# A four-layer graph network, layer 1's second attention turned key-major, the output bias added by DMA, and launch's tests put behind the samples

## The chip, the cores and the metric

The kernel runs on one core of a Trainium2 chip. Such a core has five engines that run side by side and meet at semaphores: TensorE (PE, matmuls and transposes; its weight loads are listed as PEld), VectorE (DVE), ScalarE (ACT), GpSimd (POOL) and SyncE (SP, which here only issues DMAs). Each engine works through its own list of instructions strictly in order. The metric is the time of one execution in microseconds. Before the change the median of three runs is 4023.1 us (4022.46 to 4024.0).

## The reference

32 samples, each a matrix x of 512 nodes by 256 features, go one after the other through four residual layers. All share one 512x512 adjacency. Each layer adds a graph network of relu(layernorm(x)) to x:

```python
h = relu(layernorm(x)); x = x + L0(h)   # 4 heads: softmax over neighbours of q.k/8, then out @ wo.T + bo
h = relu(layernorm(x)); x = x + L1(h)   # relu(h @ mlp1), attention over all nodes, mlp2, attention over neighbours
h = relu(layernorm(x)); x = x + L2(h)   # 4 heads of additive attention, elu
h = relu(layernorm(x)); x = x + L3(h)   # 8 heads of additive attention with a prior, @ W_out.T
```

The change is about the additive attention of layer 1, `_gat(inp, adj, W, a)`:

```python
h = inp @ W;  f1 = h @ a[:F];  f2 = h @ a[F:]
e = leaky_relu(f1[i] + f2[j], 0.2);  e = -9e15 where adj[i, j] is 0
out = elu(softmax_j(e) @ h)
```

Layer 1 does it twice: `first_gat` without a mask on 512 features, `second_gat` with the mask on 256. Both results go through a second elu and get their input added.

## The kernel before, in words

All arithmetic is float32. A sample's 512 nodes are four tiles of 128 partitions (`NT = 4`), its 256 features two (`KD = 2`). A scratch tile of 128x512 is a *block* (57 of them in SBUF), and a PSUM tile of the same size a *bank* (8). A feature-major tile has features on its partitions and nodes along its row; a node-major tile has it the other way round.

**Launch (lines 424 to 601).** Loads go out on the queues of SP, ScalarE and GpSimd. The adjacency is converted to float and turned by 16 transposes (496). Four masks come from it. The projections of the attention vectors on the weights of layers 2 and 3 are computed (480 to 487), as are bias columns (566), `boa` (587, 595: output bias of layer 0, with the value bias carried through wo) and `b2a` (592, 596). *Tests* bound the sizes of the scores (524 to 582). Their verdict `go` is loaded into a register on every engine (1367), and a branch (1368) leads to `pipelined`, which runs here, or to `general`, a slower path for inputs that the bounds do not admit. The samples' own loads stand behind that branch.

**The samples (`pipelined`).** The code of the four layers doesn't issue instructions. A recorder (`q.vector`, `q.tensor` and so on) collects each operation as a step. `Plan.order` (156) then puts all steps of all samples into one order. For each step it works out the earliest start from the engine's time, from the steps that it depends on, from free blocks and banks, and from a release time (`STARTS`, `PACE`, `LAYERS`); among steps it takes the one with the earliest start and, between equals, the earliest due time: the sample's number times `PERIOD`, less the length of what hangs on the step, less a value out of `URGENT`. Durations in this planner come from `cost` (311). `issue` (265) emits the steps in that order, each on its engine, and beyond the first 100 steps slips in one of launch's leftovers (`late`: 8 products over W_fc, 4 over W_hand, 4 mask products) at every other step. So nearly every instruction of the samples carries one line, 275, in the profile, and is told apart by the tiles that it writes and reads. On TensorE, units of matmuls that use row halves or column strips of the array are kept together (`q.unit`).

**Layer 0 (733 to 779).** Norm, transposes, q, k and v; per head pair and key tile scores, an exponential, a mask product and running sums; then weighted sums. `normalise` (708) sends the sums through DRAM and back to get their reciprocals on all partitions. At 776 four GpSimd additions put `boa` onto x, and two VectorE additions add the product with wo.

**Layer 1, first attention (781 to 840).** It is key-major: a tile p[j] has the 128 keys of j on its partitions and all queries along its row. With d the largest f2 of all nodes, the softmax weight is a maximum of two products, each of a factor of the query and a factor of the key. The query's factor is put on all partitions by four transposes and a copy, the sums over keys are taken from a total by four transposes and a reduction, and their reciprocals are spread again by four transposes (`rc`).

**Layer 1, second attention (842 to 880).** It is query-major: queries on the partitions, keys along the row.

```python
q.tensor.transpose(fb[:, col(t)], v[:, t, D + 1 : D + 2].to_broadcast([P, P]), ident)   # f2 on all partitions
q.scalar.activation(s, fb, AF.Identity, bias=v[:, t, D : D + 1])                        # + f1
q.vector.scalar_tensor_tensor(s, s, ALPHA, s, op0=ALU.mult, op1=ALU.max)                # leaky relu
q.vector.tensor_tensor_reduce(out=p[t], in0=s, in1=mask1[:, t, :], ...)                 # mask, row minimum of -e
q.scalar.activation(p[t], p[t], AF.Exp, bias=nm[:, t : t + 1], scale=-1.0, accum_out=sm[:, t : t + 1])
q.vector.reciprocal(r[:, t : t + 1], sm[:, t : t + 1])
q.scalar.mul(p[t], p[t], r[:, t : t + 1])
```

The weighted sum needs keys on the partitions, so 16 transposes and four copies (pT, 864 to 868) turn p.

**Layers 2 and 3 (`separable`, 902).** Key-major; a query row R per head comes back from DRAM (rd) on all partitions. Per head and key tile there is one exponential on ScalarE and one masked maximum on VectorE. Part of the sums is added by accumulating DMAs that GpSimd issues (p<-p). The last samples take sums on TensorE instead (`direct`).

Of the kernel before, what the change touches and what calls it, by code (L numbers as in the profile page):

```python
# [39 lines left out]

PERIOD = 57.0
STARTS, PACE = (0.0, 11.0, 54.0, 70.0), 29.0
LAYERS = (0.0, 55.0, 178.0, 198.0)

URGENT = {
    "h:0": 49, "pt:0": 23, "mm:0": 7, "sc:0": 89, "p0:0": -655, "total:0": -158, "av:0": -3, "rc:0": -39,
    "oT:0": -103, "stats:1": 94, "h:1": 11, "pt:1": 6, "hT:1": 93, "mm:1": -5, "r1:1": -511, "total:1": -50,
    "rs1:1": -41, "av:1": -24, "o2:1": -243, "fb:1": -11, "s:1": 20, "r2:1": 94, "pt:2": 134, "mm:2": -7,  # L50
    "p3:2": -20, "av:2": -185, "total:2": -319, "sm:2": -35, "ue:2": -200, "stats:3": 6, "ms:3": -69,
    "h:3": -156, "hT:3": 112, "mm:3": -58, "e8:3": -19, "p3:3": -989, "av:3": -489, "total:3": -598,
    "raw:3": -11,
}
BLOCKS, KEEP = 57, 2
KEEP_BANKS = 0

LATE = 100
BANKS = ("mm", "av", "sm", "sc", "pt", "fb")
# [10 lines left out]
class Plan:  # L70
# [85 lines left out]
    def order(self):  # L156
# [16 lines left out]
        free = {tag: [0.0] * bufs for tag, (bufs, _) in self.tags.items()}  # L173
        held = {}
# [136 lines left out]
def cost(engine, op, args, kw, out):  # L311
# [22 lines left out]
    if engine == "POOL":  # L334
        if op == "dma_start":
            return 1.1, 5.2
        return (1.0 if n < 16 else 0.683), 0.1
# [7 lines left out]
def gnn_stack_kernel(ctx: ExitStack, tc: tile.TileContext, a: dict, out: bass.AP):  # L345
# [21 lines left out]
    def load_rows(name, eng, cols):  # L367

        src = a[name]
        k = src.shape[0] // P  # L370
        t = const.tile([P, k, cols], F32, name=name)
        eng.dma_start(t[:, :, : src.shape[1]], T(src, "(k p) c -> p k c", p=P))
        return t
# [5 lines left out]

    def load_bcast(pool, name, eng, n):  # L380
        t = pool.tile([P, n], F32, name=name)
        load(t, name, eng)
        return t
# [12 lines left out]
    go = const.tile([1, 1], I32, name="go")  # L396
    bq8 = const.tile([P, KD], F32, name="bq8")
# [11 lines left out]
    mask1 = const.tile([P, NT, N], BF16, name="mask1")  # L409
# [3 lines left out]

# [6 lines left out]
    afc = first.tile([P, 2 * HID], F32, name="afc")  # L420
    ahd = first.tile([P, 2 * D], F32, name="ahd")
    prf = first.tile([P, HID], BF16, name="prf")
# [3 lines left out]
    with prep_stack, tc.manual_schedule():  # L426
# [5 lines left out]
        nc.scalar.dma_start(w2[:, :, H2 : H2 + D], T(a["L2_W"], "(k p) c -> p k c", p=P))  # L432
        src = a["L2_a"]
        a2 = prep.tile([P, 2, F2], F32, name="a2")
        nc.scalar.dma_start(a2, bass.AP(tensor=src.tensor, offset=src.offset, ap=[[0, P], [1, 2 * F2]]))
        for k in range(KD):
            nc.gpsimd.dma_start(
                T(w3[:, k, H3 : H3 + D], "p (h f) -> p h f", h=H3), T(a["L3_W"][:, k * P : (k + 1) * P, :], "h p f -> p h f")
            )
        bt = load_bcast(prep, "beta", nc.scalar, 1)  # L440
# [8 lines left out]
        wq = load_rows("wqT", nc.scalar, D)  # L449
        wk = load_rows("wkT", nc.sync, D)  # L450
        s3 = load_bcast(prep, "L3_a_src", nc.sync, D)
        d3 = load_bcast(prep, "L3_a_dst", nc.sync, D)
        m2 = load_rows("mlp2_w", nc.sync, D)
        wo = load_rows("woT", nc.sync, D)
        bo = load_bcast(prep, "bo", nc.sync, D)
        wv = load_rows("wvT", nc.sync, D)
        m1 = load_rows("mlp1_w", nc.sync, HID)
        wfc = load_rows("W_fc", nc.sync, HID + 2)
        f1a, r1a = wfc[:, :, HID : HID + 1], wfc[:, :, HID + 1 :]
        load(afc, "a_fc", nc.sync)  # L460
        wh = load_rows("W_hand", nc.sync, D + 2)
        load(ahd, "a_hand", nc.sync)
        w3o = load_rows("L3_WoT", nc.sync, D)

# [4 lines left out]
        one = prep.tile([P, 1], F32, name="one")  # L469
        nc.vector.memset(one, 1.0)  # L470
        H = H2 + H3
        tests = prep.tile([P, 2 * H + 5], F32, name="tests")
        nc.vector.memset(tests, 0.0)


        def project(w, kn, heads, f, vec, dst):

            for k in range(kn):
                pr = prep.tile([P, heads, f], F32, name="pr")
                nc.vector.tensor_tensor(pr, T(w(k), "p (h f) -> p h f", h=heads), vec, op=ALU.mult)  # L480
                nc.vector.tensor_reduce(dst(k), pr, axis=AX.X, op=ALU.add)

        def projections(w, h, f, vs, vd):
            project(lambda k: w[:, k, h : h + D], KD, h, f, vs, lambda k: w[:, k, :h])
            project(lambda k: w[:, k, h : h + D], KD, h, f, vd, lambda k: w[:, k, 3 * h + D :])
            nc.vector.tensor_scalar(w[:, :, h + D : 2 * h + D], w[:, :, :h], ALPHA - 1.0, None, op0=ALU.mult)
            nc.vector.tensor_scalar(w[:, :, 2 * h + D : 3 * h + D], w[:, :, 3 * h + D :], ALPHA, None, op0=ALU.mult)


        top = prep.tile([P, NT], F32, name="top")  # L490
# [6 lines left out]
        at = [prep.tile([P, N], F32, name="at", bufs=NT) for _ in range(NT)]  # L497
        m3 = [mask3T[:, j, :] for j in range(NT)]
        for j in range(NT):
            nc.scalar.copy(at[j], adjT[j])  # L500
            nc.scalar.activation(m3[j], adjT[j], AF.Relu)
        projections(w2, H2, F2, a2[:, 0:1, :].to_broadcast([P, H2, F2]), a2[:, 1:2, :].to_broadcast([P, H2, F2]))

        ab = prep.tile([P, 1], F32, name="ab")
        nc.vector.tensor_scalar(ab, bt, -1.0, None, op0=ALU.mult)
        nc.vector.tensor_tensor(ab, ab, bt, op=ALU.max)
        nc.scalar.activation(ab, ab, AF.Exp, scale=-1.0)
        nc.scalar.activation(ab, ab, AF.Ln, bias=one)
        for j in range(NT):
            nc.scalar.activation(m3[j], m3[j], AF.Ln, bias=eps)  # L510
        projections(w3, H3, F3, T(s3, "p (h f) -> p h f", h=H3), T(d3, "p (h f) -> p h f", h=H3))
        nc.vector.scalar_tensor_tensor(beta, bt, 0.0, ab, op0=ALU.max, op1=ALU.add)

        grams = []
        for w, name in ((wq, "bq"), (wk, "bk")):
            gp = pp.tile([64, N], F32, name="gp", bufs=2)
            for h in range(4):  # L520
                c = slice(h * 64, (h + 1) * 64)
                r = row[:, spans[name] + h * 64 : spans[name] + (h + 1) * 64]
                for k in range(KD):
                    nc.tensor.matmul(gp[:, c], w[:, k, c], w[:, k, c], start=(k == 0), stop=False)
                nc.tensor.matmul(gp[:, c], r, r, start=False, stop=True)
            gram = prep.tile([64, D], F32, name="gram", bufs=2)
            nc.vector.tensor_copy(gram, gp[:, :D])
            grams.append(gram)
        gp = pp.tile([64, N], F32, name="gp", bufs=2)
        for n in range(2):  # L530
            for h in range(4):
                c = slice(h * 64, (h + 1) * 64)
# [892 lines left out]
```

## Time and profile before

| | |
|---|---|
| median of three runs | 4023.1 us |
| the profiled execution | 4023.19 us |
| its span, first to last instruction | 4021.3 us |
| granted TensorE clock, mean | 0.994 |
| the chain that ended last, shares of the span | products mm 30%, weighted sums av 19%, transposes pt 5% |
| largest work on VectorE | masked maxima of layer 3, 715.2 us in 1024 |
| HBM traffic | 44 GB/s over the span |

The profile is one execution. A line of groups gives the engine, the operation, the tile written and the tiles read, the shapes and the count; then the busy time of all and the mean duration of one in ns; then how long the engine sat idle just before them and which instruction ended that. A matmul of float32 data is listed as two records, a transpose as one. Records of TensorE overlap, so busy time over count says what one adds, and the mean what one takes from start to end. A table by stage has, for each stretch, its length, the busy time of PE, PEld, DVE, ACT and POOL with counts, the granted clock, the DMA share and GB/s.

### The profile page before, as it was taken

To read this page: it belongs to the slowest core of one execution; us is meant where nothing else is said; L and a number is where in the kernel's file an instruction comes from. 1 tells how busy PE (TensorE), PEld (TensorE's weight loads), DVE (VectorE), ACT (ScalarE), POOL (GpSimd) and SP (SyncE) were. 2 spreads that over 40 slices of the span, in tenths; PEclk is the share of its full clock that TensorE was granted. 3 is DMA by queue.
4 is the path that set the end of the run, shared out by engine and by line. 5 is a ranking of instruction groups with operands and counts; after the bars stand their busy time and mean duration, and the time that the engine had idled before them with its cause. 6 is when DMAs were issued, how large, how long until landed. Compare 5 with 4: busy or idle time off the path is not lost.

```text
span 4021.3 us, 53382 instructions
## 1 busy us (share of the span) xinstructions
PE 3933.0 (98%) x17366; PEld 2179.0 (54%) x17366; DVE 3303.2 (82%) x6940; ACT 2992.8 (74%) x6386; POOL 659.0 (16%) x636
## 2 busy tenths in 40 slices
PE   8999999999999999999999999999999999999997
PEld 4655555555555655555555555655555555555553
DVE  6478888788888888888788887888888788887877
ACT  4568687877788777877877788777877777787766
POOL 2101110212121021110211211021110211111110
PEclk9999999999999999999999999999999999999998
DMA  2003231323332132322322323133322322322331
GB/s 81 17 17 90 64 85 54 80 64 69 75 80 72 46 90 63 74 70 67 86 64 61 82 65 87 47 71 73 83 69 67 85 64 59 78 70 71 65 79 49
DMA packets 198018, 274.80 MB, mean 68 GB/s; under 512 B 47273, under 2 KB 84394, under 8 KB 197730
## 3 DMA queue, kind: packets, MB, share of 16 engines
q1 hardware_dynamic: 144832, 176.05, 14.2%
q0 software_dynamic: 52064, 94.66, 13.8%
q8 instruction: 139, 2.28, 0.2%
q14 instruction: 149, 1.22, 0.1%
q10 hardware_dynamic: 834, 0.59, 0.1%
HBM read 157.74 MB, written 19.10 MB: 44 GB/s over the span
## 4 chain that ended last, share of the span: by engine, by line
PE 60%; DVE 17%; ACT 5%; DMA 4%; POOL 3%; issue 2%; SPq 0%; DVEq 0%; ACTq 0%; POOLq 0%
PE mm L275 30%; PE av L275 19%; PE pt L275 5%; DVE p L275 4%; PE sm L275 3%; PE sc L275 3%; DVE total L275 3%; ACT p L275 2%; POOL rs L275 2%; DVE x L275 2%; DVE stats L275 2%; DMA p<-p 2%; DVE ue L275 2%; DVE o L275 1%; DMA rc<-s 1%
## 5 line engine op out<-in xcount | busy, mean ns | idle before, releaser
L275 ACT ACTIVATE p<-R,e 128x512 f32<-128x512 f32 x1536 | 1005.4, 731 | 108.0 <-PE av L275 73.7
L275 DVE SCALAR_TENSOR_TENSOR p<-p,e,mask3T 128x512 f32<-128x512 f32 x1024 | 715.2, 741 | 179.5 <-ACT p L275 179.0
L275 PE MATMUL av<-p,v 128*128 128x512 f32 (+1 forms) x2048 | 700.5, 597 | 2.6 <-DVE p L275 2.5
L275 POOL TENSOR_TENSOR rs<-ve,mhalf 128x4 f32<-128x4 f32 x128 | 216.3, 1689 | 2214.4 <-DVE ve L275 1761.9
L275 DVE TENSOR_TENSOR total<-total,p 128x512 f32<-128x512 f32 x808 | 527.6, 683 | 0.8
L275 PE MATMUL av<-p,vs 128*32 128x512 f32 (+1 forms) x3072 | 491.0, 598 | 5.3 <-DVE p L275 5.3
L275 POOL DMA_DIRECT2D p<-p x360 | 323.0, 1095 | 1049.3 <-DVE p L275 412.9
L275 PE MATMUL mm<-W_fc,o 128*128 128x256 f32 (+1 forms) x2048 | 482.0, 381 | 4.9 <-ACT o L275 4.7
L275 PEld LDWEIGHTS av<-p,v 128*128 128x128 f32 (+1 forms) x2048 | 256.1, 163 | 348.5 <-issue 299.4
L275 PEld LDWEIGHTS mm<-W_fc,o 128*128 128x128 f32 x2048 | 375.4, 190 | 88.9 <-ACT o L275 22.3
L275 DVE TENSOR_TENSOR p<-p,mask0T 128x512 f32<-128x512 f32 x512 | 329.5, 680 | 65.0 <-ACT p L275 65.0
L275 DVE SCALAR_TENSOR_TENSOR p<-p,e,mask1T 128x512 f32<-128x512 f32 x512 | 355.0, 742 | 4.6 <-ACT p L275 4.3
L275 ACT ACTIVATE h<-x,ms,rs 128x256 f32<-128x256 f32 x512 | 276.8, 602 | 76.1 <-DVE ms L275 67.8
L275 PEld LDWEIGHTS av<-p,vs 128*32 128x32 f32 (+1 forms) x3072 | 133.1, 118 | 323.8 <-issue 238.2
L275 DVE TENSOR_TENSOR total<-p,p 128x512 f32<-128x512 f32 x404 | 279.7, 710 | 12.3 <-DMA p<-p 7.6
L275 ACT COPY v<-mm 128x256 f32<-128x256 f32 (+2 forms) x384 | 170.0, 452 | 138.7 <-PE mm L275 107.0
L275 ACT ACTIVATE p<-sc 128x512 f32<-128x512 f32 x512 | 256.1, 618 | 15.7 <-PE sc L275 15.5
L275 PE MATMUL mm<-w,hT 128*128 128x272 f32 (+1 forms) x1024 | 253.7, 395 | 8.0 <-ACT hT L275 8.0
L275 PE MATMUL mm<-hT,mlp_w 128*128 128x512 f32 x512 | 242.2, 600 | 2.4 <-ACT hT L275 1.5
L275 PE MATMUL sc<-qT,kT 64*128 64x512 f32 x1024 | 241.1, 606 | 0.2 <-ACT p L275 0.2
L275 PE MATMUL mm<-o,mlp_w 128*128 128x512 f32 x512 | 238.0, 594 | 0.0
L275 PE MATMUL av<-pT,v 128*128 128x512 f32 x512 | 226.6, 593 | 0.1
(189 smaller groups left out, 5977.3 us busy)
## 6 DMA issues: line engine op xcount, KB each, us to landing
R<-rd SPq DMA_DIRECT2D x384, 256.0 KB
p<-p POOLq DMA_DIRECT2D x360, 256.0 KB, 5.3
x<-in_x_dram SPq DMA_DIRECT2D x32, 512.0 KB
rc<-s SPq DMA_DIRECT2D x128, 128.0 KB
out_dram<-x SPq DMA_DIRECT2D x32, 512.0 KB
rc<-s SPq DMA_DIRECT2D x248, 64.0 KB
s<-sums SPq DMA_DIRECT2D x94, 8.0 KB
few<-s SPq DMA_DIRECT2D x94, 8.0 KB
```

The lines of the kernel that those rows point to most:

```text
L275: getattr(getattr(self.nc, attribute), op)(*args, **kw)
```

## The change

The diff touches four things.

- **Second attention** becomes key-major like the first. `largest`, `on_all`, `inverse_sums` and `elu2` are taken out of `first_gat` and shared. The mask is the transposed one; the products with `rc` come after the weighted sums. A condition on the spread of f2 in each sample is new (`spread`).
- **Output bias**: one DMA per sample, issued by GpSimd, accumulates `boa` into x; it is held until v is written.
- **Launch**: only the adjacency, x of sample 0 and q, k and v are loaded ahead of the samples, and only two masks and the bias columns are made. All other loads and preparations (`preparation`) are slipped in between the samples' steps from the 30th on. The tests become steps of a 33rd sample of the plan (`tests`). The branch comes behind everything: `pipelined` always runs, and `general` runs behind it if the verdict is against.
- **The planner's numbers**: PERIOD, STARTS, PACE, LAYERS and URGENT, 62 blocks for 57, ten of them held back until its time 120.

```diff
-PERIOD = 57.0
-STARTS, PACE = (0.0, 11.0, 54.0, 70.0), 29.0
-LAYERS = (0.0, 55.0, 178.0, 198.0)
+PERIOD = 134.0
+STARTS, PACE = (0.0, 0.0, 82.0, 163.0), 113.0
+LAYERS = (0.0, 48.0, 0.0, 189.0)
 URGENT = {
-    "h:0": 49, "pt:0": 23, "mm:0": 7, "sc:0": 89, "p0:0": -655, "total:0": -158, "av:0": -3, "rc:0": -39,
...
+    "pt:0": 166, "mm:0": 75, "sc:0": 126, "total:0": 49, "pt:1": 25, "mm:1": 40, "nd:1": 9, "p1:1": 126,
+    "total:2": -404, "ue:2": -193, "mm:3": -135, "p3:3": -681, "av:3": -684, "total:3": -608,
 }
-BLOCKS, KEEP = 57, 2
+BLOCKS, KEEP = 62, 2
-LATE = 100
+LATE = 30
+FILLED, FILLED_TO = 10, 120.0
...
         free = {tag: [0.0] * bufs for tag, (bufs, _) in self.tags.items()}
+        free["block"][:FILLED] = [FILLED_TO] * FILLED
...
+        x0 = new_x()
+        nc.sync.dma_start(x0, xv[0])
...
+            q.behind(v[1])
+            q.gpsimd.dma_start(out=xt, in_=boa[:, None, :].to_broadcast([P, NT, D]), accum_op=ALU.add)
...
-            for t in range(NT):
-                q.gpsimd.tensor_tensor(xt[:, t, :], xt[:, t, :], boa, op=ALU.add)
...
+        def on_all(name, cols):
+            pt, b = bank("pt"), block(name)
+            for t in range(NT):
+                q.tensor.transpose(pt[:, col(t)], cols[:, t : t + 1].to_broadcast([P, P]), ident)
+            q.scalar.copy(b, pt)
+            return b
+        def largest(d):
+            mx, nd, pt = small("mx", 1), small("nd", 3), bank("pt")
+            q.vector.reduce_max(mx, d, axis=AX.X)
+            q.tensor.transpose(pt[:, :P], mx.to_broadcast([P, P]), ident)
+            q.vector.reduce_max(nd[:, 0:1], pt[:, :P], axis=AX.X)
+            q.vector.tensor_scalar(nd[:, 1:2], nd[:, 0:1], -1.0, None, op0=ALU.mult)
+            q.vector.tensor_scalar(nd[:, 2:3], nd[:, 0:1], -ALPHA, None, op0=ALU.mult)
+            return nd
+        def inverse_sums(p):
+            total = block("total")
+            q.vector.tensor_tensor(total, p[0], p[1], op=ALU.add)
...
+            rc = on_all("rc", rs)
+            q.behind(sm)
+            return rc
+        def elu2(dst, av, rc, residual):
+            y = block("y")
+            q.vector.tensor_tensor(y, av, rc, op=ALU.mult)
...
         def second_gat(o3):
...
-                q.scalar.mul(p[t], p[t], r[:, t : t + 1])
-            pT = blocks("pT", NT)
             for j in range(NT):
-                pt = bank("pt")
-                for t in range(NT):
-                    q.tensor.transpose(pt[:, col(t)], p[t][:, col(j)], ident)
-                q.scalar.copy(pT[j], pt)
...
+            d = v[:, :, D + 1]
+            nd, mn, ew = largest(d), small("mn", 1), small("ew2", 3, NT)
+            q.vector.tensor_reduce(mn, d, axis=AX.X, op=ALU.min)
+            q.vector.tensor_tensor(spread[:, q.sample : q.sample + 1], nd[:, 0:1], mn, op=ALU.subtract)
+            q.vector.tensor_scalar(ew[:, 2, :], v[:, :, D], nd[:, 0:1], 0.0, op0=ALU.add, op1=ALU.max)
+            q.vector.tensor_scalar(ew[:, 1, :], d, ALPHA, nd[:, 2:3], op0=ALU.mult, op1=ALU.add)
+            q.scalar.activation(ew[:, 0, :], d, AF.Exp, bias=nd[:, 1:2])
+            r, p = on_all("r2", ew[:, 2, :]), blocks("p2", NT)
+            for j in range(NT):
+                q.scalar.activation(p[j], r, AF.Exp, bias=ew[:, 1, j : j + 1], scale=ALPHA - 1.0)
+                q.vector.scalar_tensor_tensor(
+                    p[j], p[j], ew[:, 0, j : j + 1], mask1T[:, j, :], op0=ALU.max, op1=ALU.mult
+                )
+            rc = inverse_sums(p)
             yT = blocks("yT", KD)
             for m in range(KD):
+                elu2(yT[m], weighted([v[:, j, col(m)] for j in range(NT)], p), rc, o3[m])
...
+        q.begin()
+        q.layer = 3
+        tests()
+        late = preparation(
...
         q.issue(tc, late)
+        with tc.manual_schedule():
+            narrow = spread[:, 0:1]
+            nc.vector.reduce_max(narrow, spread, axis=AX.X)
+            nc.vector.tensor_scalar(narrow, narrow, SAFE_SPREAD, None, op0=ALU.is_le)
+            tp = psum.tile([P, N], F32, tag="bank", name="tp", bufs=8)
+            nc.tensor.matmul(tp[:1, :1], ones[:, 0:1], narrow, start=True, stop=True)
+            nc.vector.tensor_scalar(narrow[:1, :], tp[:1, :1], P - 0.5, None, op0=ALU.is_gt)
+            nc.vector.tensor_tensor(go1, go1, narrow[:1, :], op=ALU.mult)
+            nc.vector.tensor_copy(go, go1)
...
+    with ExitStack() as stack:
+        pipelined(stack)
     fits = nc.values_load(go[0:1, 0:1])
-    with tc.If(fits > 0) as either:
-        with ExitStack() as stack:
-            pipelined(stack)
-    with either.Else():
+    with tc.If(fits < 1):
         with ExitStack() as stack:
             general(stack)
```

## The prediction

> **What bounds the kernel now.** I read the page's first two parts first: which engine is busy, and whether that holds over the whole span.
>
> ```profile
> span 4021.3 us, 53382 instructions
> PE 3933.0 (98%) x17366; PEld 2179.0 (54%) x17366; DVE 3303.2 (82%) x6940; ACT 2992.8 (74%) x6386; POOL 659.0 (16%) x636
> PE   8999999999999999999999999999999999999997
> ```
>
> TensorE is busy 98% of the span, and only the first and last slice fall below nine tenths. VectorE at 82% is next. So a microsecond taken from TensorE is worth about one, and a microsecond added elsewhere costs nothing while that engine has room. Where are TensorE's 88.3 idle us? The table by stage answers (after the stretch and its length: PE, PEld, DVE, ACT, POOL busy):
>
> ```profile
> 0.00:39.50 39.50, 25.24 (x126) 21.04 (x126) 22.06 (x81) 14.31 (x24) 19.75 (x21) 1.00 0.60 192
> 39.50:140.00 100.50, 96.44 (x364) 51.28 (x365) 57.31 (x140) 49.87 (x99) 18.09 (x20) 1.00 0.07 22
> 600.00:3600.00 3000.00, 2981.47 (x13216) 1659.25 (x13213) 2546.10 (x5325) 2299.61 (x4930) 509.32 (x483) 1.00 0.30 70
> 3880.00:4021.30 141.30, 107.39 (x523) 52.64 (x521) 91.24 (x180) 86.79 (x185) 3.39 (x3) 0.86 0.17 56
> ```
>
> Idle: 14.3 us in launch, 4.1 behind it, 18.5 in the 3000 us of the middle, 33.9 in the tail. Of launch's 39.5 us no part is sample work. Third, the groups by form give prices; I divide busy time by count, since the mean of one includes overlap:
>
> ```profile
> L275 PE MATMUL pt<-ident,p 128*128 128x128 f32 x512 | 69.5, 282 | 4.3 <-ACT p L275 3.6 <-ACT pT L275 0.7
> L275 PE MATMUL fb<-ident,v 128*128 128x128 f32 x128 | 23.3, 276 | 0.0
> L275 PE MATMUL pt<-ident,ew 128*128 128x128 f32 x128 | 19.2, 272 | 0.0
> L275 PE MATMUL sc<-qT,kT 64*128 64x512 f32 x1024 | 241.1, 606 | 0.2 <-ACT p L275 0.2
> L275 DVE SCALAR_TENSOR_TENSOR p<-p,e,mask1T 128x512 f32<-128x512 f32 x512 | 355.0, 742 | 4.6 <-ACT p L275 4.3
> L275 POOL DMA_DIRECT2D p<-p x360 | 323.0, 1095 | 1049.3 <-DVE p L275 412.9 <-ACT e L275 347.4 <-PE av L275 92.6
> ```
>
> A 128x128 transpose costs TensorE 0.14 to 0.18 us.
>
> **Second attention, TensorE.** Out go 16 transposes of p a sample (69.5 us in all) and 4 of f2 (23.3): 92.8. In come, a sample, 4 each of ew, total and rs (the first attention's rows: 19.2 us per 128, so 57.6) and one of the maximum (8.7 per 32): 66.3. Net **-26.5**, all on TensorE.
>
> **Second attention, the other engines.** VectorE loses s (82.3), the masked minimum with its accumulator (83.7 + 10.3), r (19.8) and yT's two steps (42.8 + 41.6): 280.5. It gets 128 steps at 355.0/512 = 0.69 (89), 96 adds at 0.65 (63), 64 products with rc at 0.68 (43), elu's two steps at 0.72 and 0.75 (94), and small steps (rs 21.9 + 4.7, maxima, minimum and negations some 25, ew 14): about 355. So +75, or 2.3 us a sample; VectorE then does about 3380 us against TensorE's 3890, 87%. ScalarE loses s, p's exponential and accumulator, the scaling and pT (81 + 92 + 27 + 84 + 66 = 350), gets 128 exponentials (84), two copies a sample (38) and small ones (10): -218. I take both at nothing: TensorE covers them. If VectorE became last everywhere, its 75 would be added; nothing excludes part of that.
>
> **Array changes.** In the built order TensorE passes 386 times between full matmuls, row halves and column strips; the new order 295 times. The price from sc: inside one unbroken run (32 records in 7.06 us at 2000 us) a record takes 0.2206; on average 241.1/1024 = 0.2354. The excess, 15.2 us, over 61 runs is 0.25 a run, 0.125 for each of its two borders. 91 fewer: **-11**; the ends are 0 (the excess is something else) and -23 (all of it at one border).
>
> **Output bias.** 128 POOL additions go (113.7 us, 0.93 each); 32 accumulating DMAs come, each waiting on POOL for the four h and v. Issue by the p<-p row is 1.1 us, 35 in all, on an engine at 16%; behind a waiting issue stand the powers of the next norms, as they stood behind the additions. [...] The row's slowest issue in a stretch of 60 us at 2000 us is 1.88 us; at that price it is 60 us, still below 113.7. Landing: 5.3 us for 256 KB, so at most 10.6 for 512; the addition that needs it comes after the whole of layer 0's attention. Zero by both; up to +5 if a power is held up now and then, no gain, since POOL bounds nothing.
>
> **Launch.** First sample transposes begin at 39.52 now. The chain was: adjacency in (last cast 11.15), tests, go at 30.05, x's load issued 30.72, stats 35.39. After, x is loaded right behind the adjacency. In the built order the first stats wait for TensorE's 12 bias matmuls, whose rows come by POOL's DMAs (issued by 5.9, about 6 us to land: 11). Those matmuls took 23.32 to 28.6, 5.3 us: 16.3. From stats to transposes was 4.13, now with four mask steps (1.43) and a bias copy between: about 22. So **-17**; ends -11 (loads late) and -25 (x in at 10.5 and nothing else waits).
>
> What launch loses goes elsewhere. boa's and b2a's matmuls (2.08 + 3.41) come into layer 0, and the tests' matmuls (12.68 to 23.32, 10.6 us) some 100 us ahead of the end, where TensorE is still full. By these rows +16. [...] The trace shows that although the granted clock reads 1.00: q and k passes start 0.85 apart at 44 us, 0.43 from 46 us on. So beside busy work these cost half: **+8**; ends +4 and +16.
>
> Into the first samples also go VectorE's projections (8 products, 8 reductions: 8.2 us), mask and beta steps (3.5), and ScalarE's logarithms, exponentials and table loads (8.2). The W_fc and W_hand steps were there already. Cover is short: from 60 to 100 us VectorE was busy 39.9 of 40, and TensorE lost 2.6. At full exposure +12; I take half, +6. In the new order sample 2 starts on TensorE at its 169th step instead of the 74th, sample 3 at the 358th instead of the 197th. So layer 0's way through DMA (sums to oT: 3960.1 to 3976.0 in the tail, 16 us) and layer 1's norm have only one other sample as cover. I take +5. Together **+11**, ends 0 and +30.
>
> **End.** The last samples overlap as before: the same steps, and one unit less of sample 30 beside sample 31's layer 3. The go of all samples (about six small steps of 0.15 to 0.3 and one matmul) and the branch (go to next issue: 0.67 us at launch) take some 2.5 us behind the last x at 4017.41, beside the output's DMA, which ends the span 3.9 us later. **+1**; ends 0 and +4. The adjacency reductions for the tests (some 8 us of VectorE) I take at nothing, for room in the last 400 us.
>
> **Sum.** -26.5 - 11 - 17 + 8 + 11 + 1 = -34.5. The profiled execution took 4023.2 us, within 0.1 of the median 4023.1, so **3989**.
>
> **Rivals.**
> 1. Launch's gain is eaten by its own work: the first 150 us stall for the full 30 instead of 11. For: the full VectorE and few samples. Against: PE was busy 96.4 of 100.5 us there while W_fc's steps ran. Gives 4008; chance 0.18.
> 2. The new order also closes idle time: of the 10.7 us idle from 140 to 600 and 18.5 in the middle, most go because ScalarE is lighter by 7 us a sample and 62 blocks replace 57; with half of that and launch at -25: 3989 - 15 - 8 = 3966, to 3950 with array changes at -23. Against: the middle idles 0.6%, so there is little to win. Chance 0.18.
> 3. Slower: VectorE becomes last. Its place is layer 1's second attention beside another sample's layer 3, where VectorE has 32 masked steps of 0.69 and 12 additions, about 30 us, against some 20 of TensorE. Each us of VectorE's extra 75 then goes to the span: 3989 + 75 = 4064 if everywhere; with seven tenths 4041. It decides once VectorE ends last in about half (34.5/75) of the samples. Against: VectorE keeps 13% free, and TensorE waited for p from VectorE only 7.8 us in all. Chance 0.12.
>
> **The numbers.** The likeliest (0.52) is 3989, its own range 3975 to 4003. Below 3952 I leave part of rival 2 out, above 4018 most of rival 3: range 3952 to 4018. A measurement of this kernel can tell 0.2%, 8 us, from no change. Faster: 0.52 + 0.18 + 0.14 of rival 1 = 0.84; within: 0.04 of rival 1, 0.02 of rival 3 = 0.06; slower: 0.10.
>
> **What would show it.** PE busy near 3885 with the p transposes gone and 128 more each of ew, rs and total; first h transposes near 22 us; idle of PE under 25 us in the first 200; VectorE near 3380, ScalarE near 2780; idle in the middle still under 1%. PE idle of some 70 us in the middle with releaser VectorE would be rival 3. The prediction is wrong if idle per 200 us in the middle rises over 3, or if the first matmuls come after 30 us.

## The result, and the profile after

The changed kernel took 3979.08 us, the median of four runs (3977.9 to 3979.61), beside 4022.78 for the kernel before (also four runs): a ratio of 0.9893, 95% interval 0.9876 to 0.991. That is 43.7 us less; 34.5 less was forecast. The profiled execution's span is 3977.5 us, 43.8 below the one before.

The page first. The three lines answer to the three that the prediction began with:

```profile
span 3977.5 us, 52568 instructions
...
PE 3888.6 (98%) x17144; PEld 2146.2 (54%) x17144; DVE 3341.5 (84%) x7049; ACT 2807.2 (71%) x5968; POOL 563.8 (14%) x530
...
PE   7999999999999999999999999999999999999986
```

TensorE is still the bound: 3888.6 us busy (3885 was expected), 44.4 less than before, and every slice between first and last two is at nine tenths or more. VectorE went up by 38 us and ScalarE down by 186; neither engine bounds the span. The table by stage (length, then busy PE, PEld, DVE, ACT, POOL, then clock, DMA share, GB/s) says where TensorE is idle:

```profile
0.00:39.50 39.50, 27.85 (x118) 18.68 (x120) 18.43 (x67) 14.48 (x26) 7.70 (x14) 0.83 0.78 218
39.50:140.00 100.50, 83.23 (x318) 44.60 (x315) 58.70 (x136) 42.10 (x84) 3.04 (x3) 0.90 0.05 17
140.00:600.00 460.00, 458.35 (x1965) 254.62 (x1964) 379.43 (x798) 324.17 (x690) 59.22 (x54) 1.00 0.26 63
600.00:3600.00 3000.00, 2986.33 (x13174) 1650.52 (x13174) 2587.21 (x5436) 2179.65 (x4648) 456.88 (x425) 1.00 0.32 76
```

Length less PE: 17.3 us idle from 39.5 to 140, where before had 4.1; 1.7 up to 600 (before 10.7); 13.7 in the middle (before 18.5). And the groups by form, for the second attention:

```profile
L276 PE MATMUL pt<-ident,ew 128*128 128x128 f32 x256 | 39.4, 276 | 0.9 <-DVE ew L276 0.9
...
L276 PE MATMUL pt<-ident,rs 128*128 128x128 f32 x256 | 38.9, 275 | 1.4 <-DVE rs L276 0.6
...
L276 PE MATMUL sm<-ident,total 128*128 128x128 f32 x256 | 39.1, 273 | 0.1
```

The groups of p and f2 (92.8 us before) are gone; ew, rs and total now have 256 transposes instead of 128 each. That is 20.2 + 19.7 + 19.9 more, and 8.7 for the maxima: a net of -24.3 us.

The whole difference as a ledger, from TensorE's side, out of the two profiled executions:

| | us |
|---|---|
| first sample transposes begin at 18.04 instead of 39.52 | -21.5 |
| TensorE busy behind them, 3881.7 instead of 3907.8 | -26.1 |
| idle from there to 140 us, 17.7 instead of 4.0 | +13.7 |
| idle from 140 to 3600, 15.3 instead of 29.2 | -13.9 |
| idle from 3600 to the end, 44.7 instead of 40.7 | +4.0 |
| sum | -43.8 |

Two of these lines need a closer look. The first long stall behind launch, as the timeline of the changed kernel shows it (start, duration, engine, what; in brackets the idle time before and what ended it):

```profile
48.89 0.20 ACT L554 ACTIVATE ab<-ab 128x1 f32<-128x1 f32 x1 [6.39 <-DVE ab L553]
...
50.60 2.54 ACT L557 ACTIVATE mask3T<-mask3T,eps 128x512 f32<-128x512 f32 x4
...
53.16 1.28 ACT L276 ACT_TABLE_LOAD   x1
...
54.46 0.60 ACT L276 ACTIVATE p<-sc 128x512 f32<-128x512 f32 x1
...
55.11 1.12 PE L276 MATMUL av<-p,v 128*64 128x512 f32 x2 [10.65 <-ACT p L276]
```

ScalarE had made eight p of sample 0 by 42.5 us. The ninth stands on its list behind the softplus of beta, four logarithms and two ACT_TABLE_LOADs of 1.28 us each; ScalarE itself waited 6.39 us for VectorE to prepare ab. TensorE stood for 10.65 us.

The end, before and after. In before nothing follows the last output:

```profile
4017.43 0.39 SPq L275 DMA_DIRECT2D out_dram<-x  x1
```

In the changed kernel the verdict's steps run beside it:

```profile
3966.08 0.19 PE L1039 MATMUL tp<-spread,ones 128*1 128x1 f32 x2
3966.96 0.14 DVE L1040 TENSOR_SCALAR spread<-tp 1x1 f32<-1x1 f32 x1
3967.07 0.39 SPq L276 DMA_DIRECT2D out_dram<-x  x1
3967.13 0.15 DVE L1041 TENSOR_TENSOR go<-go,spread 1x1 f32<-1x1 f32 x1
3967.31 0.14 DVE L1042 CAST go<-go 1x1 int32<-1x1 f32 x1
```

Before ended 3.9 us behind the issue of the last output (4017.43 to 4021.3), the changed kernel 10.4 us behind it (3967.07 to 3977.5). No instruction that the views list fills those microseconds. They leave out register loads, branches and drains (a DRAIN stands on every engine's list behind its last work, here with 0.01 to 3.37 us); the experiments on the end below read these from the trace itself.

### The profile page after: what moved, and what is told of

The parts are those of the page before. It is cut to its first block, busy times and chain, and to the rows that moved or that the text cites. A ratio compares the mean times of both kernels' runs of the same rounds, so it can differ in the third digit from the quotient of the medians.

```text
span 3977.5 us, 52568 instructions
## 1 busy us (share of the span) xinstructions
PE 3888.6 (98%) x17144; PEld 2146.2 (54%) x17144; DVE 3341.5 (84%) x7049; ACT 2807.2 (71%) x5968; POOL 563.8 (14%) x530
## 4 chain that ended last, share of the span: by engine, by line
PE 70%; DVE 17%; DMA 5%; ACT 4%; issue 2%; POOL 2%; SPq 1%; DVEq 0%; ACTq 0%; POOLq 0%
PE mm L276 33%; PE av L276 23%; PE sc L276 5%; PE pt L276 5%; DVE p L276 5%; DVE total L276 5%; DMA R<-rd 4%; PE sm L276 3%; POOL rs L276 2%; DVE o L276 1%; ACT p L276 1%; DVE x L276 1%; DVE ue L276 1%; DVE stats L276 1%; DVE y L276 1%
## 5 line engine op out<-in xcount | busy, mean ns | idle before, releaser
L276 ACT ACTIVATE p<-R,e 128x512 f32<-128x512 f32 x1536 | 987.7, 724 | 53.0 <-DMA R<-rd 52.9
L276 PE MATMUL av<-p,v 128*128 128x512 f32 (+1 forms) x2560 | 933.8, 598 | 13.0 <-ACT p L276 10.7
L276 POOL TENSOR_TENSOR rs<-ve,mhalf 128x4 f32<-128x4 f32 x128 | 206.5, 1613 | 2755.6 <-DVE ve L276 2202.6
L276 PEld LDWEIGHTS av<-p,v 128*128 128x128 f32 (+1 forms) x2560 | 347.6, 169 | 458.0 <-issue 367.3
L276 DVE TENSOR_TENSOR total<-total,p 128x512 f32<-128x512 f32 x872 | 573.2, 689 | 0.5
L276 PE MATMUL mm<-W_fc,o 128*128 128x256 f32 (+1 forms) x2048 | 469.0, 380 | 2.5 <-ACT o L276 2.3
L276 PEld LDWEIGHTS mm<-W_fc,o 128*128 128x128 f32 x2048 | 382.3, 190 | 86.5 <-issue 29.4
L276 DVE SCALAR_TENSOR_TENSOR p<-p,e,mask1T 128x512 f32<-128x512 f32 x512 | 347.9, 750 | 41.4 <-ACT p L276 40.7
L276 DVE TENSOR_TENSOR total<-p,p 128x512 f32<-128x512 f32 x436 | 289.2, 688 | 0.0
L276 PE MATMUL sc<-qT,kT 64*128 64x512 f32 x1024 | 228.4, 596 | 0.0
L276 PEld LDWEIGHTS mm<-w,hT 128*128 128x128 f32 x1024 | 191.3, 192 | 61.5 <-issue 14.3
L276 ACT COPY v<-mm 128x512 f32<-128x512 f32 (+2 forms) x384 | 166.1, 470 | 43.7 <-PE mm L276 40.7
```

Source lines behind the costliest of these rows:

```text
L276: getattr(getattr(self.nc, attribute), op)(*args, **kw)
```

## The experiments

All runs were timed in five rounds beside the kernel before, in three sessions on different chips. Ratios are to the kernel before of the same session, with 95% intervals.

| run | us | ratio |
|---|---|---|
| softplus later | 3980.23 | 0.9899 [0.9884, 0.9915] |
| no branch | 3970.96 | 0.9872 [0.9857, 0.9887] |
| branch not taken | 3977.8 | 0.9891 [0.9876, 0.9906] |
| early register load | 3972.69 | 0.9879 [0.9864, 0.9894] |
| bias on GpSimd | 3987.79 | 0.9916 [0.9902, 0.9929] |
| before, one bank held | 4280.65 | 1.0641 [1.0627, 1.0656] |
| attention only, bank held | 4061.14 | 1.0091 [1.0077, 1.0105] |
| attention and numbers, bank held | 4284.49 | 1.0652 [1.0637, 1.0666] |
| changed kernel, old numbers, bank held | 4438.73 | 1.1034 [1.1019, 1.1049] |
| old attention, old numbers | 4301.47 | 1.0695 [1.0681, 1.071] |
| old attention, new numbers | 4248.46 | 1.0564 [1.0549, 1.0578] |
| new attention, old numbers | 4411.5 | 1.097 [1.0955, 1.0985] |

### Is ScalarE's preparation what stalls the first sample?

My theory was that the softplus and the masks in front of the ninth p cost the 10.65 us. The edit issues the last five leftovers from step 400 on:

```diff
+LATER, LAST = 400, 5
-                if late and n > LATE:
+                if late and n > (LATE if len(late) > LAST else LATER):
```

> The kernel after, with launch's beta and logarithm steps and the mask product of layer 3 (the last five leftovers) slipped in from step 400 on instead of right behind the others. Theory: TensorE's 10.65 us wait at 44 to 55 us is ScalarE's order. Its exponential for beta waits 6.4 us for VectorE, and with two table loads and four logarithms it keeps the scores' exponentials away for 12 us[...]. Then PE idle from 39.5 to 140 falls from 17.3 to under 9 us and the time from 3979 to 3964 to 3971. Rival: the first samples lack cover whatever ScalarE does; the idle moves on, and the time stays at 3975 or above.

It took 3980.23 us, which can't be told from the changed kernel. The stall at 55 us is gone, and yet:

```profile
39.50:140.00 100.50, 91.30 (x341) 47.64 (x341) 58.59 (x141) 43.10 (x86) 3.04 (x3) 0.97 0.06 18
140.00:600.00 460.00, 451.03 (x1940) 251.55 (x1940) 377.70 (x793) 321.41 (x685) 57.10 (x53) 0.99 0.26 63
```

The first stage has 9.2 us idle instead of 17.3; the second has 9.0 instead of 1.7, in the main one wait of 7.3 us of a product for o from VectorE at 147.5 us. The theory falls: the idle time moves on and comes back. That fits the rival, too few samples under way before 150 us to fill TensorE, whichever engine is last at one place; no run put more samples there.

### What does the end cost?

Two edits: one without register load, branch and slower path, which are left out; one in which the branch is turned round, so that the usual way falls through to a small memset. Behind the memset it still jumps, unconditionally, over the slower path.

```diff
-    fits = nc.values_load(go[0:1, 0:1])
-    with tc.If(fits < 1):
-        with ExitStack() as stack:
-            general(stack)
```

> The kernel after without the register load, the branch and the slower path behind it (the verdict is computed and not used). Theory: from the issue of the last output to the end of the span 10.4 us pass against 3.9 before, and the 6.5 more are the load of go, the branch and the jump. Then the span ends some 4 us behind the last issue and the time is 3971 to 3974. Rival: it is the output's DMA, landing late; then 10 us stay, 3979.

> The kernel after with the branch turned round: a verdict in favour falls through to one small memset and an unconditional jump over the slower path, as it was before the change; a verdict against is the one that jumps on the condition. If the taken conditional jump is what costs the 6.5 us at the end: 3972 to 3975. If it is the register load, the wait for all queues or the jump as such: 3978 to 3981.

Without them the kernel takes 3970.96 us, 8 less than the changed kernel; its span ends 4.1 us behind the last output's issue (3966.08 to 3970.2), as before's did. With the branch turned round it takes 3977.8, and ends 9.8 us behind it. So the cost is real. It doesn't hang on which way the condition goes; the jump itself isn't ruled out, since this run has one too. A third edit takes verdict and register load away from the end, and leaves nothing out. The last test is issued 40 steps behind the last write of a spread and the register load 200 steps behind that write, among the last sample's steps; the branch stays last on every engine's list:

```diff
+VERDICT, LOAD = 40, 200
+                if n == last + VERDICT:
+                    verdict()
+                if n == last + LOAD:
+                    load()
-    with tc.If(fits < 1):
+    with tc.If(fits[0] < 1):
```

> The changed kernel with nothing left out: the last test (largest spread, its matmul, its product with the tests' verdict) is issued 40 steps behind the last sample's last write of its spread, and the load of the verdict into the engines' registers 200 steps behind it, between the steps of the last sample; the branch stays at the end. Theory (the load into registers at the end is the larger part of the 6.5 us): 3974, between 3972 and 3976, with the span's end some 6 us behind the last issue of an output. Rival (it is the branch, and what an engine does after it): 3979, end 10 us behind the last issue. A third outcome: the engines' loads stop TensorE in the middle of the last sample's work, and 3979 to 3985.

3972.69 us. It issues the last output so, at a span of 3970.5:

```profile
3965.46 0.39 SPq L284 DMA_DIRECT2D out_dram<-x  x1
```

5.0 us from the last issue to the end, against 10.4 and against 4.1 without any of it. Moving verdict and load takes away 5.4 of the 6.3 us. Where they lie, the records of GpSimd in the trace show (us; in brackets what an instruction took):

| GpSimd | changed kernel | branch turned round | early register load | no branch |
|---|---|---|---|---|
| loads go into a register | 3967.49 (0.49) | 3967.14 (0.49) | 3857.94 (0.49) | none |
| its branch | 3968.05 (0.05) | 3967.70 (0.05) | 3906.88 (0.05) | none |
| its jump behind the memset | none | 3968.90 (0.04) | none | none |
| next instruction on the far side | 3972.14 | 3972.25 | 3909.45 | none |
| its last drain of work | 3973.26 (3.37) | 3972.25 (3.42) | 3910.55 (3.37) | 3907.33 (4.77) |
| last output issued (SyncE) | 3967.07 | 3966.72 | 3965.46 | 3966.08 |
| end of the span | 3977.5 | 3976.5 | 3970.5 | 3970.2 |

The closing barrier of all engines comes right behind the end of that drain (3976.6 in the changed kernel), where SyncE had been ready since 3974.0. So neither the load nor the branch as such is long. What is long is the 4.0 us until GpSimd's next instruction behind the jump, and its drain of 3.4 us behind that; with the branch turned round, the jump at 3968.90 costs 3.3 us the same way. VectorE and ScalarE lose 4.0 us behind the branch too, SyncE 2.4. GpSimd has no work left from 3910 us on: with the verdict early, or without a branch, it has jumped and drained some 60 us before the others are through, and in the kernel before it drained at 3959.56. Only a verdict written at the very end makes it wait until then. What an engine does in the 4 us, the trace doesn't say. This is the fastest version that computes all that the changed kernel does.

### Was the bias DMA worth nothing?

Here the DMA is replaced by the four additions of before, held back until v is written like the DMA.

```diff
-            q.behind(v[1])
-            q.gpsimd.dma_start(out=xt, in_=boa[:, None, :].to_broadcast([P, NT, D]), accum_op=ALU.add)
+            for t in range(NT):
+                q.behind(v[1])
+                q.gpsimd.tensor_tensor(xt[:, t, :], xt[:, t, :], boa, op=ALU.add)
```

> The kernel after with the output bias added by four GpSimd additions a sample again, each held until v is written. Theory: nothing on the path, 3976 to 3984, POOL busy 80 us up. Rival: the additions slow VectorE[...] and TensorE with it: VectorE's busy time rises by 20 us or more and the time to 3985 or above.

3987.79 us: 8.7 more than the changed kernel, and each of its five runs (3984.92 and up) is slower than each of the changed kernel's four (3979.61 and down). The groups of this run:

```profile
L276 DVE TENSOR_TENSOR total<-total,p 128x512 f32<-128x512 f32 x872 | 589.2, 703 | 0.5
...
L276 POOL TENSOR_TENSOR x<-x,boa 128x256 f32<-128x256 f32 x128 | 245.7, 1944 | 8.7 <-ACT h L276 8.7
...
L276 DVE SCALAR_TENSOR_TENSOR ms<-mv,rs 128x4 f32<-128x4 f32 x128 | 36.5, 285 | 74.3 <-POOL rs L276 74.2
```

of the changed kernel, and of the kernel before:

```profile
L276 DVE TENSOR_TENSOR total<-total,p 128x512 f32<-128x512 f32 x872 | 573.2, 689 | 0.5
...
L276 POOL DMA_DIRECT2D x<-boa x32 | 46.7, 1475 | 10.1 <-ACT h L276 10.1
```

```profile
L275 POOL TENSOR_TENSOR x<-x,boa 128x256 f32<-128x256 f32 x128 | 113.7, 926 | 34.7 <-ACT h L275 33.9
```

One addition takes GpSimd 1944 ns here in the mean (half of them 1175 or less), where it took 926 in before (half of them 732 or less). VectorE does the same steps as in the changed kernel and is busy 3389.3 us instead of 3341.5; total takes 589.2 instead of 573.2, ms 36.5 instead of 20.8. So both engines take longer at once, VectorE 48 us in all beside 128 additions: in this place the additions cost VectorE time. By what way they do, the traces don't show. For the additions of the kernel before this isn't shown: they stood elsewhere in the order, and ms took VectorE no longer there (20.6 us) than with the DMA.

Where is it in the span? The first output is issued 6.0 us later than in the changed kernel (405.77 and 399.74), the last one 8.4 us later (3975.45 and 3967.07). The first 6 us are a later start (first transposes at 21.53 instead of 18.04) and a longer first stall (13.18 us instead of 10.65). The late start is not the additions' doing, since three runs without them start at 20.57 to 20.83. Nor does it last: these three are 2.8 to 3.9 us behind at the first output, and 0.4 to 1.6 ahead at the last. So a late start is no rival for the 8.7 us, and most of them go with the additions. That VectorE's 48 us are what makes them is argued from the two engines' times, not shown by a run of its own.

### What is each part worth by itself?

The first try put the parts of the change onto the kernel before. With the planner's setting of before, the new attention found no order that its buffers allow, so one bank was held for the oldest sample in these four runs (`KEEP_BANKS = 1`), with a control. In the two runs on the kernel before, the condition on the spread is left out.

> A control: the kernel before with one PSUM bank held for the oldest sample in the planner (the next three need that to be ordered at all). 4015 to 4031.

> The control with only layer 1's second attention made key-major; launch, bias, branch and the planner's other numbers as before; the condition on the spread of f2 is left out. Theory: TensorE's transposes decide, 24 to 27 us less than the control, about 3997. Rival 1: the order with its array changes and closed waits is what gained; then 0 to 12 less. Rival 2: VectorE's additional work comes through; then no less than the control.

> The one before this with the new planner numbers too (period, starts, pace, release of layers, urgency), still 57 blocks and the old launch. Theory: fewer array changes on TensorE take another 8 to 14 us, about 3986. Rival: the numbers only suit the new launch, and nothing is gained, 3997 or more.

> The kernel after with the planner numbers of before (62 blocks kept, one bank held for the oldest sample). Theory: the array changes come back and cost 8 to 14 us, and idle in the middle grows by some us: 3988 to 3998. Rival: the order is worth nothing, 3977 to 3983.

The control broke the plan: with nothing changed but that one reserve, the kernel before took 4280.65 us, 257 more than without it in the same session. The same matmuls keep TensorE busy 4055.2 us instead of 3933.0, and it is idle 226 us instead of 88. Against that control the other three say nothing about attention or numbers: 219 less, 4 more, 158 more. They are inconclusive, except for the size of what they ran into.

The second try needs no bank held. It starts from the changed kernel and puts back the query-major attention (mask built in launch, spread set to zero: that condition is left out), the old planner numbers, or both. The number of blocks could not be held fixed: 57, 60 and 59, against 62.

```diff
-PERIOD = 134.0
-STARTS, PACE = (0.0, 0.0, 82.0, 163.0), 113.0
+PERIOD = 57.0
+STARTS, PACE = (0.0, 11.0, 54.0, 70.0), 29.0
...
-BLOCKS, KEEP = 62, 2
+BLOCKS, KEEP = 59, 2
```

> The changed kernel with the second attention put back to query-major (its node-major mask is built in the launch by GpSimd, its spread condition is left out: the spread is set to zero) and with the planner numbers and the 57 blocks of the kernel before, and no bank held: so the kernel before plus launch, moved tests, bias by DMA and branch at the end. Theory (the parts add): 4023 - 21.5 (first transposes) + 13.7 (stalls of the first sample) + 2.9 (moved matmuls) + 6.5 (end) - 9 (bias) = 4016, between 4008 and 4024. Rival (what the order of the work costs is a term of its own, and moves with any edit): more than 15 us away from 4016 on either side, with TensorE idle for another amount than 29 us between 140 and 3600 us.

> The changed kernel with the second attention alone put back to query-major (mask built in the launch, spread condition left out), planner numbers of the changed kernel, 60 blocks in place of 62. Theory (attention is worth what its matmuls take off TensorE, some 24 us): 3979 + 24 = 4003, between 3998 and 4010, TensorE idle in the middle as in the changed kernel (15 us between 140 and 3600). Rival (the numbers were fitted to the new attention): 4040 or more, the difference as idle time of TensorE in the middle.

> The changed kernel with the planner numbers of the kernel before, no bank held, 59 blocks in place of 62. Theory (the numbers are worth the 11 us of array changes and the 14 us of idle time): 3979 + 25 = 4004, between 3990 and 4015. Rival (the numbers belong to the attention; the earlier run with a bank held kept most of its loss): 4040 or more, as idle time of TensorE in the middle, in waits for probabilities and for their transposes.

All three went the rivals' way, and much further than I had set them: 4301.47, 4248.46 and 4411.5. With launch, tests, bias and branch as changed, the four combinations are:

| | old numbers | new numbers |
|---|---|---|
| old attention | 4301.5 | 4248.5 |
| new attention | 4411.5 | 3979.1 |

Each entry also has its own number of blocks (57 and 60 above, 59 and 62 below), so "numbers" here means numbers with their blocks; what two to three blocks do alone was not run. With 62 blocks but one bank held, the old numbers took 4438.73 us. The attention is worth -269 us under the new numbers and +110 under the old ones. The numbers are worth -432 us with the new attention and -53 with the old. And the kernel before, which differs from the upper left corner by launch, tests, bias, branch and the planner's settings for the start (ten blocks held back, leftovers from step 30 on), took 4022. A part has no price of its own here. What kind of time is it? The page and the waits of TensorE (what it waited for, us in total, times, longest) from 140 to 3880 us, for the new attention under old numbers:

```profile
PE 4075.8 (92%) x17144; PEld 2195.2 (50%) x17144; DVE 3366.3 (76%) x7049; ACT 2831.5 (64%) x5968; POOL 560.7 (13%) x530
```

```profile
PE av L280 <- DVE p L280: 61.3, 37, 3.8
PE pt L280 <- DVE yT L280: 45.0, 11, 5.2
PE pt L280 <- ACT h L280: 41.5, 28, 5.8
PE mm L280 <- DVE oT L280: 25.0, 13, 5.8
```

and the changed kernel's own, whose matmuls are the same 17144:

```profile
PE mm L276 <- ACT o L276: 7.9, 17, 1.1
PE pt L276 <- ACT h L276: 5.2, 2, 5.1
```

No engine but TensorE (92%) is busy over four fifths of the longer span: VectorE 76%, ScalarE 64%. TensorE waits a few us at a time for products of every layer (p and oT of the attentions, yT of layer 1, h of a norm). At 1600 us one sees how:

```profile
1608.40 4.27 PE L280 MATMUL av<-p,vs 128*32 128x512 f32 x12 [2.15 <-DVE p L280]
1613.43 1.71 PE L280 MATMUL av<-p,vs 128*32 128x512 f32 x4 [0.77 <-DVE p L280]
1616.23 1.10 PE L280 MATMUL mm<-woT,oT 128*128 128x256 f32 x4 [1.10 <-DVE oT L280]
1621.17 2.54 PE L280 MATMUL av<-p,vs 128*64 128x512 f32 x4 [3.84 <-DVE p L280]
```

VectorE had been busy 38.9 of the 40 us up to 1600 and is busy only 26.0 of the next 40, ScalarE 29.4. TensorE's list holds nothing at that place but steps of layer 3 (p with mask3T), layer 0 (woT) and layer 2 (p with mask1T), of three samples, then; and each is the end of a chain that is not through yet. For layer 2, ScalarE itself waits 4.71 us at 1619 for a row R out of DRAM. So work piles up on VectorE before this place and is missing at it. I read that as the order's doing, not an engine's capacity; it is one place, and no run shows it for all the waits.

With the idle time came slower matmuls. Against the changed kernel, with the same matmuls, this run is idle 247.5 us more, and TensorE is also busy 187.2 us more (4075.8 - 3888.6). Its mean granted clock is 0.963 instead of 0.990. The run with old attention under new numbers shows one case:

```profile
1236.39 3.46 PE L276 MATMUL mm<-o,mlp_w 128*128 128x512 f32 x4 [6.83 <-DVE o L276]
...
1241.42 4.03 PE L276 MATMUL mm<-o,mlp_w 128*128 128x512 f32 x9
```

with the table's rows for the two stretches (the third number from the end is the granted clock):

```profile
1236.40:1239.70 3.30, 3.30 (x5) 1.37 (x6) 2.37 (x6) 1.72 (x4) 1.34 (x1) 0.54 0.12 40
1239.70:1242.00 2.30, 2.30 (x13) 1.53 (x12) 2.27 (x11) 0.95 (x3) 0.00 (x0) 1.00 0.03 7
```

Behind 6.83 us of idle time four records take 3.46 us, 0.87 each; nine records 5 us later take 4.03, 0.45 each. The granted clock is 0.54 in the first stretch and 1.00 in the second, so the half pace that the prediction read at launch (passes 0.85 us apart, then 0.43, at a recorded clock of 1.00) is seen behind this stall too. It doesn't explain all of the 187 us: the two mean clocks over the two spans make some 123 us of missing clock (an estimate, part of it in idle stretches), and 125 more array changes at 0.093 us, a price worked out below, make 12. The rest stays open.

Which of the old numbers does the harm was not separated, and it isn't known whether other numbers would have served the old attention as well.

## Why the prediction was right, point by point

The direction, the bound and the size were right. The sum came close partly by luck: its terms missed by 22 us on one side and by 13 on the other, and one assumption carried it unsaid. The profiled executions, in the prediction's own terms:

| us | forecast | measured |
|---|---|---|
| second attention on TensorE | -26.5 | -24.3 |
| array changes, at the price found below | -11 | -8.5 |
| launch | -17 | -21.5 |
| matmuls moved out of launch | +8 | +10.5 |
| idle time of the first samples | +11 | +13.7 |
| idle time from 3600 us to the end | +1 | +4.0 |
| idle time from 140 to 3600 us | 0 | -13.9 |
| all other matmuls, as what is left | 0 | -3.8 |
| sum | -34.5 | -43.8 |

- **Second attention.** No run isolates the -24.3, for the reason above. It is read from the groups, and it appears in the span because TensorE stayed full.
- **Array changes.** The count was right: the timelines of TensorE pass 386 times between full matmuls, row halves and column strips before, and 295 times after. The price of 0.125 us was too high. It came from a group's busy time over its count, which in short runs also counts the overlap with the neighbour. From start to start the traces show it directly. In before,

```profile
1996.85 3.62 PE L275 MATMUL mm<-wvT,hT 128*128 128x256 f32 x16
2000.40 7.14 PE L275 MATMUL sc<-qT,kT 64*128 64x512 f32 x32
```

  16 records of 256 columns last 3.55 us until the row halves begin; inside such a run one lasts 0.216, so 16 would last 3.46, and 0.09 is added. Over all starts between 200 and 3600 us the median behind a full record goes from 0.109 to 0.203 (transposes, to column strips) and from 0.216 to 0.309 (256 columns, to row halves), and that behind a strip or half of 512 columns is 0.52, where 0.43 is the pace of full records of 512. So a change costs 0.093 us, and 91 fewer save 8.5, an estimate from count and price.
- **Launch.** The chain was right: rows, bias matmuls, stats, transposes. -21.5 is a lucky execution. The 24 records of the bias matmuls took 3.04 us (from 8.54, at a granted clock of 1.00); four other runs with this launch have 5.28, as was taken over from before, and begin their transposes at 20.57 to 21.53, so they gain 18 to 19. Only the run without branch (2.83, 17.68) is like the profiled one. And the three late starters above make these 3 us good by the last output, so not all of launch's gain reaches the end.
- **Moved matmuls.** boa's and b2a's took 1.03 and 1.84 us, those of the tests 7.4 by their groups, 0.2 the last test's: 10.5, where the rows of launch had 16 and the prediction took half.
- **First samples.** The preparations that I gave half of it to are seen in the stall, but taking ScalarE's part away gave nothing back. That fits the other half, too few samples under way; it isn't shown.
- **End.** This step failed. The text took go and branch at 2.5 us beside the output's DMA, from the 0.67 us between go and the next issue at launch. That issue is SyncE's alone, and at launch TensorE still had b2a's matmuls until 34.3 us. At the end GpSimd's way behind the verdict (load 0.5, jump 4.0, drain 3.4) outlasts the output's DMA, and the end grew by 6.5 us: in that place the forecast was 5.5 us too low. The rest of the tail closed by 2.5.
- **Output bias, zero ("no gain, since POOL bounds nothing").** Against additions behind v this is wrong: with them the kernel is 8.7 us slower, though POOL bounds nothing, and VectorE's steps get longer. Against the additions of before, where they stood, no run tests it.
- **VectorE +75, ScalarE -218.** They were +38 and -186. On VectorE the new steps took some 342 us instead of 355, and some 23 came off elsewhere, as o<-o,o (96.4 to 87.9) and layer 2's masked maxima (355.0 to 347.9). Why is open: with the additions put back VectorE is at +86, but these groups stay as short (87.4, 346.4), so the DMA isn't shown to have relieved them.
- **Idle time in the middle.** The forecast left it alone and gave rival 2, that half of it closes, a chance of 0.18. About half did close, 13.9 of 29.2 us. So a part of rival 2 came true; no run tells whether lighter ScalarE, more blocks or the order did it. (By its own terms rival 2 reaches down to 3954, not 3950.)
- **What was not priced.** The steps assumed that TensorE would stay full in the new order, because the middle idled 0.6% before. That was true, but not for a reason that the prediction gave: an order by other numbers, with three blocks fewer, costs 432 us for the same steps. The rival on the slow side was VectorE becoming last everywhere. The danger that the runs found was an order in which TensorE's list at some place holds only ends of unfinished chains, while no other engine is over 80% over the span. The built order would have been the place to look for that; I took only the array changes from it.

## What to carry to other kernels

Where a planner writes the order of in-order engines, the order is a term of its own, here up to ten times the change's gain, and here it suited only the list of steps that it was made for: a part undone under the other's numbers tells about the numbers. Read from the built order which samples stand at which stage together before pricing instructions. A verdict that decides a branch at the end is best computed and loaded into registers while the last work still runs, so that an engine that is done early can take its jump and its drain then: here that took away 5.4 of 6.3 us.

## What the runs showed of the hardware that was not expected

- Behind a branch over the slower path, the engines' next instructions came 2.4 to 4.0 us later, though the register load took 0.5 us and the branch 0.05 to 0.07 (3.73 in TensorE's record); GpSimd's drain behind it took 3.4. With the verdict written at the very end this cost 6.3 us (10.4 against 4.1 behind the last issue), with verdict and load among the last sample's steps 0.9.
- A change between full matmuls, row halves and column strips costs TensorE 0.093 us from start to start, before and after the change alike.
- 128 GpSimd additions of 128x256 went with 48 us more of VectorE's time and took 1944 ns each where they stand behind v (926 in before, at another place); as 32 accumulating DMAs they take GpSimd 46.7 us of issue.
- In five profiled orders with more idle time, TensorE was also busy longer, by 0.4 to 1.0 us for each us of added idle time: 187 on 247 (new attention, old numbers) and 226 on 232 (the same with one bank held), against the changed kernel; 69 on 156 (old attention, new numbers), 99 on 172 (old attention, old numbers) and 122 on 138 (before, one bank held), against the kernel before. At the one place shown, behind a stall of 6.83 us, the granted clock was 0.54 and a record took 0.87 us instead of 0.45; that is a part of it.
